# Two transformer blocks: the first FFN matrix product in pairs of elements, as seven block products instead of eight

## The chip, the core and the metric

The kernel runs on one core of a Trainium2 chip. The metric is the device time of one execution in microseconds (us). A core has five engines that work side by side, each through its own instructions in order: TensorE (PE in the profile; the loading of its weights is PEld), VectorE (DVE), ScalarE (ACT), GpSimd (POOL) and SyncE (SP), which in this kernel does nothing but issue DMAs. Where an instruction waits for another engine, all that stands behind it on its own engine waits too.

## What is computed

The input `x` holds 16 elements of 256 tokens by 256 channels, all in fp32. It passes through two layers, and each layer has three parts: self-attention, cross-attention to `ctx_768`, and an FFN. Cut to the part that is changed:

```python
# layer 0 (layer 1 likewise, with weights, norms and modulation of its own)
ffn_in = layernorm(x) * (1.0 + g(cond)) + b(cond)      # per element
h = gelu(ffn_in @ ff_w1 + ff_b1, approximate=False)    # 256 -> 1024
x = h @ ff_w2 + ff_b2 + x                              # 1024 -> 256
```

The pairs of factor and addend (the "modulation") come from one conditioning vector per element.

## The kernel before

The work is cut into six phases: self-attention, cross-attention and FFN of layer 0 (p0, p1, p2), then those of layer 1 (p3, p4, p5). A phase goes through the 16 elements, b0 to b15. An attention job has two steps and an FFN job four, s = 0 to 3. One loop over all steps writes the orders of all engines by hand (`manual_schedule`): what the loop calls first comes first on each engine it touches.

**Preparing an element.** An element's input goes through a chain on several engines. `prepare_moments` takes mean and variance on DVE. `prepare_norm` takes the root on GpSimd (L330), normalizes on DVE (L338), turns 32x32 blocks on DVE (L348) and makes SP issue four DMAs to DRAM (L353, `turned`). `prepare_fetch` makes SP issue four DMAs back (L363, `fetched`). `prepare_input` applies factor and addend, one half on ACT (L396) and one on GpSimd (L397), and leaves `hT`, channels on the partitions. All DMAs of the kernel are issued from SP in program order.

**The FFN before.** The first matrix stands as two tiles `w10` and `w11` (L82's `w_a` in layer 0 and `w_b` in layer 1). `ffn_hidden(job, s)` makes 256 of the 1024 outputs for the 256 tokens of one element in one PSUM bank. `product` (L82) is one 128x128 weight block against a row of columns, written as four matmuls of 32 outputs. Two gelus on ACT (L704) move the bank to SBUF. After four steps the element has its 1024 hidden values. The output product of the element before is made meanwhile: `fold_inner` (L736) adds up five combinations of hidden blocks on DVE at s0, and `finish_folded` (L738) makes seven block products with them at s2 and adds the result to `x` on DVE (L750 to L757). Its weights are combined once for a phase by `fold_weights` (L727, five DVE additions, at s1 of b0). So the output product already takes seven block products for eight; the hidden product takes all eight.

**The borders.** The last element of cross-attention of layer 0 has its sums made (`sum_up`) and its rows scaled (`scale`, L627) while the first FFN elements run; its output product (`finish`, L775) comes at FFN b1, s3. The last self- and FFN products of a phase are made in the next phase's first steps.

**The modulations of layer 1.** Three times in layer 0's FFN, at b2, b5 and b8, a modulation is made: its weights are loaded by SP at s0; at s3 16 matmuls (L199), a copy on ACT (L204), a transpose on DVE (L206) and 16 small DMAs issued by SP (L210, `turned_b`). They are put to use one element later (DVE, L173 to L177). The sixteen are issued so:

```python
for q in range(4):
    for g in range(4):
        nc.sync.dma_start(out=turned[32 * q : 32 * q + 32, g // KC, g % KC, :],
                          in_=blocks[32 * g : 32 * g + 32, q, 0:NB])
```

In the four steps of an FFN element the loop calls, for the elements ahead:

```python
if s == 1 and after is not None:
    prepare_fetch(after)          # two ahead
if s == 1 and third is not None:
    prepare_moments(third); prepare_norm(third)
if s == 3 and after is not None:
    prepare_input(after)
```

## Time and profile before

| what | value |
|---|---|
| median of 3 runs | 2196.24 us (2194.89 to 2197.59) |
| profiled execution | 2198.64 us |
| its span | 2196.8 us |
| granted TensorE clock, mean | 0.999 |
| layer 0: self-attention, cross-attention, FFN | 615, 638, 213 us |
| layer 1: both attentions, FFN | 472, 217 us |

The span is what the hardware profiler shows of the execution, from the first to the last instruction; the profiled execution's own time is 1.84 us longer. The five stages follow each other from about 42 us on; before that the weights and constants arrive. The profile's page gives for each engine its busy time and share, and for each group of instructions its line, its operation with output and input tile, the count, the mean duration and the idle time ahead of it. In a timeline a row is a run of like instructions: start, duration, engine, line, operation, count, and in brackets the idle time before and who ended it. Every matmul of the program shows as two records.

### The profile page before, as it was taken

The page shows a single profiled execution, that of the slowest core. Times are in us where ns is not written, and L with a number is a line of the kernel's source. Part 1 is how long each engine was busy: PE and PEld are TensorE (multiplying, and loading weights), DVE is VectorE, ACT ScalarE, POOL GpSimd, SP SyncE. Part 2 cuts the span into 40 slices and gives each one's busy share as a digit, 9 for nine tenths or more (in the row PEclk, how much of TensorE's full clock was granted, in tenths as well). Part 3 has the DMA queues.
Part 4 walks back from the last instruction along what each step waited for, and adds up shares of the span by engine and source line. Part 5 has one row for each costly group of instructions (what it writes and reads, how often), then busy time and mean ns, then how long its engine had stood idle before and what let it go on. Part 6 is the DMA issues. An engine that isn't in the chain of part 4 may idle for free.

```text
span 2196.8 us, 110836 instructions
## 1 busy us (share of the span) xinstructions
PE 2180.7 (99%) x50505; PEld 1431.6 (65%) x50505; DVE 1660.6 (76%) x3120; ACT 837.5 (38%) x1307; POOL 1071.6 (49%) x1033
## 2 busy tenths in 40 slices
PE   9999999999999999999999999999999999999998
PEld 5666666666665666666665668776656656657887
DVE  5886776777788899888899876664777777777654
ACT  3323323323233333333323332234666666663322
POOL 3766656656657867676676752221222232222220
PEclk9999999999999999999999999999999999999999
DMA  6110110110132221221212123221221232223221
GB/s 192 47 39 22 24 40 23 24 41 22 26 85 72 67 65 35 47 54 40 60 35 59 26 71 88 46 54 29 62 43 42 55 93 59 62 52 86 61 62 37
DMA packets 309321, 117.83 MB, mean 54 GB/s; under 512 B 245652, under 2 KB 292073, under 8 KB 308713
## 3 DMA queue, kind: packets, MB, share of 16 engines
q1 hardware_dynamic: 308840, 110.64, 21.1%
q8 instruction: 397, 6.50, 1.2%
q14 instruction: 84, 0.68, 0.1%
HBM read 77.14 MB, written 33.29 MB: 50 GB/s over the span
## 4 chain that ended last, share of the span: by engine, by line
PE 91%; DVE 3%; POOL 2%; DMA 1%; issue 1%; SPq 0%; ACT 0%; DVEq 0%; POOLq 0%; ACTq 0%
PE banks L82 59%; PE banks L569 15%; PE banks L638 9%; PE banks L654 5%; PE banks L505 1%; PE banks L472 1%; DVE m L526 1%; POOL raw L627 1%; POOL qk L534 1%; DMA spread<-sums_seen 0%; POOL folded L736 0%; DMA sums_seen<-inv 0%; DVE both L590 0%; DVE rows L603 0%; DVE squares L596 0%
## 5 line engine op out<-in xcount | busy, mean ns | idle before, releaser
L581 ACT ACTIVATE pr<-banks 128x1024 f32<-128x1024 f32 x576 | 487.6, 937 | 416.7 <-PE banks L569 211.5
L534 POOL TENSOR_TENSOR qk<-m,m 128x512 f32<-128x512 f32 x256 | 347.5, 1377 | 307.7 <-DVE m L526 199.6
L526 DVE TENSOR_TENSOR m<-banks,rope 128x512 f32<-128x512 f32 x512 | 324.2, 679 | 86.4 <-POOL qk L534 80.8
L590 DVE TENSOR_TENSOR both<-pr 128x512 f32<-128x512 f32 x256 | 222.7, 884 | 107.7 <-ACT pr L581 107.4
L645 ACT COPY raw<-banks 128x512 f32<-128x512 f32 x128 | 75.1, 587 | 468.6 <-PE banks L638 443.3
L569 PE MATMUL banks<-qk 32*64 32x256 f32 x8192 | 241.4, 378 | 4.0 <-DVE x L753 2.8
L638 PE MATMUL banks<-pr,v 128*32 128x256 f32 x4096 | 233.2, 379 | 0.0
L569 PEld LDWEIGHTS banks<-qk 32*64 32x64 f32 x8192 | 184.9, 131 | 64.6 <-issue 28.7
L704 ACT ACTIVATE g<-banks,cols 128x256 f32<-128x256 f32 x256 | 106.4, 472 | 273.0 <-PE banks L82 261.4
L638 PEld LDWEIGHTS banks<-pr,v 128*32 128x32 f32 x4096 | 132.9, 110 | 88.6 <-ACT pr L581 0.7
L82 PE MATMUL banks<-folded_w,folded 128*32 128x128 f32 x5856 | 176.2, 273 | 1.7 <-POOL folded L736 1.1
L627 POOL TENSOR_TENSOR raw<-raw,spread 128x512 f32<-128x512 f32 x128 | 162.8, 1304 | 19.0 <-DMA spread<-sums_seen 17.7
L82 PEld LDWEIGHTS banks<-folded_w,folded 128*32 128x32 f32 x5856 | 164.0, 110 | 3.1 <-POOL folded L736 2.2
L596 DVE STREAM_TRANSPOSE squares<-both 128x1024 f32<-128x1024 f32 x128 | 159.4, 1245 | 4.4
L603 DVE TENSOR_REDUCE rows<-squares 128x32 f32<-128x1024 f32 x128 | 155.5, 1215 | 2.2
L689 POOL TENSOR_TENSOR oT<-oT,spread 128x256 f32<-128x256 f32 x64 | 45.7, 736 | 209.8 <-DVE spread L688 209.8
L654 PE MATMUL banks<-pr,wide_v 128*32 128x256 f32 x2048 | 134.4, 379 | 1.1 <-ACT pr L581 1.1
L82 PE MATMUL banks<-hT,wk_sa 128*32 128x256 f32 x2048 | 135.3, 382 | 0.0
L330 POOL TENSOR_TENSOR rstd<-ve,neg_half 128x2 f32<-128x2 f32 x95 | 73.3, 772 | 125.9 <-DVE ve L328 122.5
L423 POOL TENSOR_TENSOR x<-x,bo_b 128x256 f32<-128x256 f32 x96 | 73.2, 782 | 125.8 <-DVE xh L338 125.8
L82 PE MATMUL banks<-hT,wq_ca 128*32 128x256 f32 x2048 | 133.9, 379 | 0.0
L82 PE MATMUL banks<-hT,wq_sa 128*32 128x256 f32 x2048 | 133.9, 379 | 0.0
(162 smaller groups left out, 3667.0 us busy)
## 6 DMA issues: line engine op xcount, KB each, us to landing
turned<-blocks SPq DMA_DIRECT2D x380, 64.0 KB
fetched<-turned SPq DMA_DIRECT2D x380, 64.0 KB
spread<-sums_seen SPq DMA_DIRECT2D x128, 128.0 KB
x<-in_x SPq DMA_DIRECT2D x16, 256.0 KB
fetched_c<-turned_c SPq DMA_DIRECT2D x64, 64.0 KB
cT<-in_ctx_turned SPq DMA_DIRECT2D x16, 256.0 KB
out<-x SPq DMA_DIRECT2D x16, 256.0 KB
ctx<-in_ctx SPq DMA_DIRECT2D x16, 192.0 KB
```

Of the source, the lines that this page charges most:

```text
L82: nc.tensor.matmul(out[cut], lhsT[:, cut], rhs, start=start, stop=stop)
L526: nc.vector.tensor_tensor(m, pq, rope[:, s : s + 1, :].to_broadcast([P, 2, N]), ALU.mult)
L534: nc.gpsimd.tensor_tensor(r, x, y, (ALU.subtract, ALU.add)[out])
L569: nc.tensor.matmul(banks[64 * g : 64 * g + 64, at + h, t * N : (t + 1) * N], lhs, rhs, start=(half == 0), stop=(half == 1 or job["layer"] ...
L581: nc.scalar.activation(pr[:, one], sc[:, one], AF.Exp, scale=0.125 if job["layer"] == 0 else 0.25)
L590: nc.vector.tensor_tensor(job["both"][:, 2 * p : 2 * p + 2, :], pr[:, :, 0, :], pr[:, :, 1, :], ALU.add)
L596: nc.vector.transpose(job["squares"].rearrange("p b k -> p (b k)"), job.pop("both").rearrange("p h n -> p (h n)"))
L603: nc.vector.tensor_reduce(job["rows"][:, u, :], job.pop("squares"), AX.X, ALU.add)
L627: nc.gpsimd.tensor_tensor(part, part, spread[:, u : u + 1, :].to_broadcast([P, 2, N]), ALU.mult)
L638: nc.tensor.matmul(o[32 * h : 32 * h + 32, half, :], v[:, t, col : col + 32], prs[h // 2][:, h % 2, t, :], start=(t == 0), stop=(t == NT - 1),
L654: nc.tensor.matmul(o[32 * h : 32 * h + 32], v[:, t, 4 * c + h, 32 * e : 32 * e + 32], prs[h // 2][:, h % 2, t, :], start=(t == 0), stop=(t ...
L704: nc.scalar.activation(g[:, c, :], ph[:, c, :], AF.Gelu, bias=column(w["b1"], 2 * u + c))
```

## The change

The FFN elements go in pairs (b0 and b1, b2 and b3, and so on), eight pairs in each layer, and a pair's eight steps are q = 0 to 7. The two elements' `hT` stand side by side in one tile. The hidden product is cut in two by two blocks: the 1024 outputs in two halves j, the 256 inputs in two halves k, the 256 tokens of each element in two halves t. One `block` is 512 outputs by 128 inputs by 128 tokens of both elements, four `product`s or 16 matmuls of 256 columns, in two banks. Seven blocks replace eight, named here A1 to A7 in the order of a steady pair: A1 at q0 (in the banks `main`), A2 at q0 (`side`, banks 6 and 7), A3 at q0 (`other`), A4 at q1, A5 at q3, A6 at q5 and A7 at q6. `main` and `other` change places from pair to pair. Around them:

- `split_weights`: four sums of 128x512 weight blocks on GpSimd, once for each layer; `split_input`: four sums of 128x256 on GpSimd per pair, made at q4 and q6 of the pair before.
- `kept` copies of running sums in `main` from PSUM to SBUF on ACT, and `join`s on DVE that add a bank to such a copy and leave the hidden values before gelu.
- gelus then run on SBUF, in halves: those of outputs 0 to 511 one pair later (q0 and q1), those of outputs 512 to 1023 at q3 and q6.
- The output products of a pair's elements come at q2 and q4 of the next pair, in banks 0 and 1 and with an order of their own; `fold_inner` is divided, three sums on DVE and two on GpSimd. After the last pair both elements' products follow each other.
- Fetches and inputs of the elements ahead move: in a steady pair the next pair's first element is fetched at q0 and its input made at q2, the second's at q3 and q4. `enter_ffn` at the last step of an attention phase prepares the first pair and fetches the third element.
- The first pair has no output products of its own phase behind it; its A6 comes at q1, its A3 at q5, `fold_weights` at q3. The last pair has A3 at q1, and its output products of the pair before at q4 and q7.
- The late output product of cross-attention moves to the second pair's q1. The modulations are made at q2 of the pairs of b2, b4 and b6. The product of the last but one FFN element of layer 0 moves to layer 1's first attention phase as a plain product.

The core of the diff:

```diff
+        into = None
+        if job["kind"] == "ffn":
+            if b % 2 == 0:
+                job["pair"] = work.tile([P, KC, 2, N], F32, tag="v", name=f"hT_{key}")
+            else:
+                job["pair"] = jobs[job["index"] - 1]["pair"]
+            into = job["pair"][:, :, b % 2, :]
...
-    def ffn_hidden(job, u):
...
+    def split_weights(ph):
+        w = ph["w"]
+        a = [[w[f"w1{j}"][:, k, :] for k in range(2)] for j in range(2)]
+        if ph["layer"] == 0:
+            s12, s34 = wtile([P, 2, 512], "wk0", "split_a0"), wtile([P, 2, 512], "wk1", "split_a1")
+        else:
+            both = wtile([P, 4, 512], "wv", "split_b")
+            s12, s34 = both[:, 0:2], both[:, 2:4]
+        s1, s2, s3, s4 = ph["split"] = s12[:, 0], s12[:, 1], s34[:, 0], s34[:, 1]
+        nc.gpsimd.tensor_tensor(s1, a[1][0], a[1][1], ALU.add)
+        nc.gpsimd.tensor_tensor(s2, s1, a[0][0], ALU.subtract)
+        nc.gpsimd.tensor_tensor(s3, a[0][0], a[1][0], ALU.subtract)
+        nc.gpsimd.tensor_tensor(s4, a[0][1], s2, ALU.subtract)
+    def input_blocks(job):
+        return [[job["pair"][:, k, :, t * P : (t + 1) * P] for t in range(2)] for k in range(2)]
+    def split_input(job, part):
+        b = input_blocks(job)
+        t = work.tile([P, 2, 2, P], F32, tag="hT", name=f"split_{job['key']}_{part}")
+        job.setdefault("split", []).extend((t[:, 0], t[:, 1]))
+        t1, t2, *_ = job["split"]
+        if part == 0:
+            nc.gpsimd.tensor_tensor(t1, b[0][1], b[0][0], ALU.subtract)
+            nc.gpsimd.tensor_tensor(t2, b[1][1], t1, ALU.subtract)
+        else:
+            nc.gpsimd.tensor_tensor(t[:, 0], b[1][1], b[0][1], ALU.subtract)
+            nc.gpsimd.tensor_tensor(t[:, 1], b[1][0], t2, ALU.subtract)
+    def gelu(job, j, cut, src=None):
+        dst = job["halves"][j]
+        for i in range(4):
+            nc.scalar.activation(
+                dst[:, i, cut], dst[:, i, cut] if src is None else src[:, i, :], AF.Gelu,
+                bias=column(job["phase"]["w"]["b1"], 4 * j + i),
+            )
+    every_token, first_half, second_half = slice(0, N), slice(0, P), slice(P, N)
+    def ffn_hidden(job, q):
+        key, ph, mate = job["key"], job["phase"], jobs[job["index"] + 1]
+        a = [[ph["w"][f"w1{j}"][:, k, :] for k in range(2)] for j in range(2)]
+        b = input_blocks(job)
+        s1, s2, s3, s4 = ph["split"]
+        odd = job["b"] // 2 % 2
+        before = jobs[job["index"] - 1]
+        pending = (jobs[job["index"] - 2], before) if before["kind"] == "ffn" else None
+        main, other, side = (2 + 2 * odd, 4 - 2 * odd, 6)
...
+        def block(at, left, right, start):
+            for i in range(4):
                 product(
-                    ph[:, c, :], w[f"w1{u // 2}"][:, k, (2 * (u % 2) + c) * P : (2 * (u % 2) + c + 1) * P], job["hT"][:, k, :],
-                    k == 0, k == KC - 1,
+                    banks[:, at + i // 2, i % 2 * N : i % 2 * N + N].rearrange("p (e n) -> p e n", e=2),
+                    left[:, i * P : (i + 1) * P], right, start and i % 2 == 0, True, True,
                 )
...
+        def join(j, t, at, kept):
+            for e, one in enumerate((job, mate)):
+                for half in range(len(kept)):
+                    n = 4 // len(kept)
+                    nc.vector.tensor_tensor(
+                        one["halves"][j][:, n * half : n * half + n, t * P : (t + 1) * P],
+                        parted(at)[:, n * half : n * half + n, e, :], kept[half][:, :, e, :], ALU.add,
+                    )
...
+        final = mate["b"] == NB - 1
+        def fold(one):
+            fold_inner(one, nc.vector, 2, 1, 6)
+            fold_inner(one, nc.gpsimd, 5, 7)
+        if q == 0:
+            for one in (job, mate):
+                one["halves"] = [
+                    work.tile([P, 4, N], F32, tag=("pr", "part")[odd], name=f"g_{one['key']}_{j}", bufs=4)
+                    for j in range(2)
+                ]
+            block(main, a[0][0], b[0][0], True)
+            job["first"] = kept("both", 0)
+            if pending:
+                gelu(pending[0], 0, every_token)
+                fold(pending[0])
+            block(side, s1, job["split"][0], True)
+            if pending and not final:
+                block(other, a[0][1], b[1][0], True)
+                join(0, 0, other, job.pop("first"))
+        elif q == 1:
+            block(main, s2, job["split"][1], False)
+            second = kept("squares", 1)
+            if pending:
+                job["second"] = second
+                gelu(pending[1], 0, every_token)
+                if final:
+                    block(other, a[0][1], b[1][0], True)
+                    join(0, 0, other, job.pop("first"))
+            else:
+                block(0, s4, b[1][1], True)
+                join(0, 1, 0, second)
+                for e, one in enumerate((job, mate)):
+                    sums = one["halves"][0][:, :, second_half]
+                    nc.vector.tensor_tensor(sums, parted(side)[:, :, e, :], sums, ALU.add)
+        elif q == 3:
+            if pending and not final:
+                fold(pending[1])
+            block(main, s3, job["split"][2], False)
+            third = []
+            for half in range(2):
+                t = work.tile([P, 2, 2, P], F32, tag="m0", name=f"kept_{key}_2{half}")
+                nc.scalar.copy(
+                    t.rearrange("p i e n -> p i (e n)"), flat(main)[:, 2 * half : 2 * half + 2, :]
+                )
+                third.append(t)
+            join(1, 1, side, third)
+            for one in (job, mate):
+                gelu(one, 1, second_half)
+        elif q == 5 and pending:
+            block(side, s4, b[1][1], False)
+            join(0, 1, side, job.pop("second"))
+        elif q == 5:
+            block(other, a[0][1], b[1][0], True)
+            join(0, 0, other, job.pop("first"))
+        elif q == 6:
+            block(main, a[1][1], job["split"][3], False)
+            if final:
+                fold(pending[1])
+                for one in (job, mate):
+                    gelu(one, 0, every_token)
+            for e, one in enumerate((job, mate)):
+                gelu(one, 1, first_half, parted(main)[:, :, e, :])
+                one["parts"] = [h[:, 2 * i : 2 * i + 2, :] for h in one["halves"] for i in range(2)]
...
-    def finish_folded(job, at):
+    def finish_folded(job, at, order):
         x, weights, hidden = xs[job["b"]], job["phase"]["folded"], job.pop("folded")
-        hurry = len(at) == 3
-        first, second, third = (bank(i, 4, P) for i in (at if hurry else (*at, at[1])))
+        first, second = (bank(i, 4, P) for i in at)
         places = {5: first[:, 0], 2: first[:, 1], 4: first[:, 2], 3: first[:, 3],
-                  1: third[:, 0], 7: second[:, 1], 6: second[:, 2]}
-        for m in (3, 6, 4, 5, 2, 1, 7) if hurry else places:
+                  1: second[:, 0], 7: second[:, 1], 6: second[:, 2]}
+        for m in order:
...
+    def enter_ffn(j):
+        prepare_fetch(jobs[j + 3])
+        prepare_input(jobs[j + 2])
+        for part in range(2):
+            split_input(jobs[j + 1], part)
+        prepare_norm(jobs[j + 4])
...
-        late = prev if not ffn else jobs[j - 2] if prev["kind"] == "ffn" else None
+        late = prev if not ffn else jobs[j - 3] if job["b"] == 2 else None
...
-        if ffn and layer0 and job["b"] in (2, 5, 8):
-            at = phases[3 + job["b"] // 3]
+        if ffn and layer0 and job["b"] in (2, 4, 6):
+            at = phases[2 + job["b"] // 2]
             if s == 0:
                 at["make_mod"] = at["mod_load"]()
-            if s == 3:
+            if s == 2:
                 make_mod = at
-        if ffn and layer0 and job["b"] in (3, 6, 9) and s == 3:
-            at = phases[2 + job["b"] // 3]
+        if ffn and layer0 and job["b"] in (3, 5, 7) and s == 3:
+            at = phases[2 + job["b"] // 2]
             at["mod"] = at["mod"]()
...
         if ffn:
...
-                stage_a(then[0], 0, next_bank())
...
+            q = s + 4 * (job["b"] % 2)
+            one = job if q < 4 else prev
+            before = jobs[one["index"] - 1]
+            previous = before["kind"] == "ffn"
+            if q in (0, 4) and third is not None and (previous or q == 4):
+                prepare_moments(third)
+            for ahead in (after if previous else third,) if q == 0 else (third,) if q == 3 and previous else ():
+                if ahead is not None:
+                    prepare_fetch(ahead)
+            if q == 0 and not previous and before["layer"] == 1:
+                normalize(before)
+            then = attention(i + 3, 1)
+            if q == 5 and then:
+                stage_a(then[0], 0, 3)
                 for t in range(NT):
-                    layer1_values(then[0], next_bank(), t)
+                    layer1_values(then[0], 2 - t, t)
+            ffn_hidden(one, q)
+            if previous:
+                for at, n in zip((4, 7) if one["b"] == NB - 2 else (2, 4), (2, 1)):
+                    if q == at:
+                        finish_folded(jobs[one["index"] - n], (0, 1), (4, 3, 2, 5, 1, 6, 7))
+            else:
+                if q == 1 and layer0:
+                    sum_up(before, 5)
+                if q == 6 and not layer0:
+                    finish(before, 0)
+                if q == 3:
+                    fold_weights(job["phase"])
+            if late is not None and q == 1:
+                finish(late, 1)
             if make_mod:
-                make_mod["mod"] = make_mod["make_mod"](next_bank())
...
+            ahead = {2: after, 4: after} if previous else {2: after, 3: third}
+            if ahead.get(q) is not None:
+                prepare_input(ahead[q])
+            if q in (4, 6) and nxt is not None and nxt["kind"] == "ffn":
+                split_input(nxt, q // 6)
+            if q == 6 and not previous and layer0:
+                scale(before)
         elif layer0:
             then = attention(i + 1, 0)
+            if leaving and s == 1 and nxt["kind"] == "ffn":
+                split_weights(nxt["phase"])
+                prepare_norm(third)
...
+            if job["p"] == 3 and job["b"] == 1 and s == 0:
+                finish(jobs[j - 3], at + 1)
...
-    fold_inner(jobs[-1], nc.vector, 6, 5, 2, 1, 7)
-    finish_folded(jobs[-1], (1, 2, 3))
+        if job["last"] and s == 3 and job["b"] == 7:
+            count_outside()
+    for n in (2, 1):
+        fold_inner(jobs[-n], nc.vector, 2, 1, 6, 7, 5)
+        finish_folded(jobs[-n], (2 * n - 4 + 4 * (n == 1), 2 * n - 3 + 4 * (n == 1)), (4, 3, 2, 1, 6, 7, 5))
```

## The prediction, written before the changed kernel ran

> **What bounds the kernel now.** I read the page's busy shares and the shares of its chain first, then timelines of the FFN stages, engine by engine. The page:
>
> ```profile
> PE 2180.7 (99%) x50505; PEld 1431.6 (65%) x50505; DVE 1660.6 (76%) x3120; ACT 837.5 (38%) x1307; POOL 1071.6 (49%) x1033
> ...
> PE 91%; DVE 3%; POOL 2%; DMA 1%; issue 1%; SPq 0%; ACT 0%; DVEq 0%; POOLq 0%; ACTq 0%
> ```
>
> TensorE is the bound: busy for 2180.7 of 2196.8 us, so work taken from it counts in full, and every wait that the new order gives it counts in full too. The change is thus a balance of saved matmuls against new waits. A timeline of layer 0's FFN around the second modulation (start, duration, engine, line, count, idle before):
>
> ```profile
> 1375.79 0.70 PE L199 MATMUL banks<-mod_b,condT 128*16 128x128 f32 x15
> ...
> 1377.57 12.24 SPq L210 DMA_DIRECT2D turned_b<-blocks_b  x16
> ...
> 1381.41 2.01 PE L82 MATMUL banks<-w_a,folded 128*32 128x128 f32 x63
> ...
> 1387.73 7.07 PE L82 MATMUL banks<-hT,w_a 128*32 128x256 f32 x125
> ...
> 1389.92 1.91 SPq L363 DMA_DIRECT2D fetched<-turned  x4
> ...
> 1394.43 2.01 PE L82 MATMUL banks<-w_a,folded 128*32 128x128 f32 x63
> ...
> 1394.54 0.60 ACT L396 ACTIVATE hT<-fetched,add_a,fac_a 128x256 f32<-128x256 f32 x1 [4.03 <-DMA fetched<-turned]
> ```
>
> Two output products begin 13.02 us apart (1394.43 - 1381.41): a steady element has no gap. SP is held for 12.24 us by sixteen tiny transfers, 0.77 us each; the fetch behind them starts when they are through, and ACT waits for it (4.03). In this order that hurts nobody, since the element fetched is needed later. The entry of layer 0's FFN, on GpSimd and DVE:
>
> ```profile
> 1283.19 5.96 POOL L627 TENSOR_TENSOR raw<-raw,spread 128x512 f32<-128x512 f32 x4
> ...
> 1285.64 2.37 DVE L590 TENSOR_TENSOR both<-pr 128x512 f32<-128x512 f32 x2
> ...
> 1289.39 1.30 DVE L590 TENSOR_TENSOR both<-pr 128x512 f32<-128x512 f32 x2
> ...
> 1295.84 0.69 DVE L775 TENSOR_TENSOR x<-banks,x 128x512 f32<-128x512 f32 x1 [1.49 <-PE banks L82]
> ...
> 1303.01 3.64 DVE L727 TENSOR_TENSOR folded_w<-w_a 128x512 f32<-128x512 f32 x5
> ```
>
> The same two additions take 2.37 us while GpSimd multiplies and 1.30 us when it has done: what GpSimd is given more of, DVE pays here.
>
> **The saving.** In the 125 records from 1387.73 on, 62.5 matmuls of 256 columns take 6.70 us up to 1394.43: 0.107 each, 0.429 a product. A hidden product of one element (64 matmuls) is 6.86, the output product the rest of 13.02, 6.16. A pair has 7 blocks of 4 products where it had 8: 4 x 0.429 = 1.72 us less, for 16 pairs -27.4. A block is 1.72.
>
> **Steady pairs.** A pair lasts 7 x 1.72 + 2 x 6.16 = 24.3 us on TensorE. DVE has in it six folds (0.64 each), two sets of output additions (2.6), joins (4 x 0.69, 4 x 0.42) and two norms (2.7), 19.2 in all; ACT about 12.6 (two copies of 1.04, two of 0.59, gelus at 0.42 and 0.27, affines); GpSimd 14 (four folds at 1.4, four splits at 0.76, affines, roots). None is over 24.3, and placed by hand the tightest operand, A3's turn behind the eight small gelus, has about 1 us to spare. I take 0; bounds 0 and +0.5 a pair.
>
> **The modulations: the decider.** In a pair that makes one, the sixteen DMAs stand at q2 and the fetch of the next pair's second element at q3, directly behind them on SP. Behind that fetch ACT and GpSimd hold its affines (q4), behind these ACT's gelus of A7 and GpSimd's splits. A1 of the next pair now reads both elements side by side, so it waits for this second one. From the modulation's first matmul to the end of that affine the trace has 1394.54 + 0.60 - 1375.79 = 19.35 us (1.78 to the first DMA, 12.35 to the fetch, 4.62 to ACT, 0.60). The third modulation gives 19.26 and the first 24.39, with four weight loads between that now come later. TensorE meanwhile has the 16 matmuls (0.65), A5, an output product, A6 and A7: 0.65 + 3 x 1.72 + 6.16 = 11.97. So it waits 7.4 us, three times: +22.2. Bounds: 5.9 each if other small waits fill 1.5 us of it, 12.4 each by the longest chain: 17.7 to 37. I take the two agreeing chains.
>
> A rule speaks for less: the Trainium skill, page "DMA: Bandwidth & Descriptors", section "Anatomy of one DMA — SWDGE (gpsimd) path", puts about 2 us on a DMA but only some 50 ns of it on dispatch. By it (an estimate, for a path that SP's queue need not share) sixteen are issued in 0.8 us, the chain is under 9 and the sum would be -10.7. The row of 12.24 for sixteen decides otherwise.
>
> **The entries.** Layer 0: TensorE enters at about 1295.3 and its seven blocks and the sums (0.4) would end at 1307.7. But four splits of the weights on GpSimd stand beside the additions (the 2.37 row), and the norm of b2 waits on DVE for a root that GpSimd makes only after L627's 5.96; so the addition that stood at 1295.84 ends at about 1300. After it DVE has moments, the joins and fold_weights (3.64), and the join of A3 stands behind them, to about 1315.5. The second pair's A1 writes A3's banks: it starts at 1315.6, +8.0 (6.5 if the splits cost DVE nothing, 10 if the output addition is later still). Layer 1: TensorE enters at 1979.7; its blocks and the attention's product (1.72) would end at 1993.4. The second pair needs b3, whose fetch is issued in the entry behind b2's and lands near 1996.7; affine and join take it to 1998.6: +5.2 (4 to 6.5).
>
> **The end.** Timeline of the last products:
>
> ```profile
> 2188.38 1.94 PE L82 MATMUL banks<-folded_w,folded 128*32 128x128 f32 x64
> ...
> 2188.72 0.42 DVE L750 TENSOR_TENSOR x<-x,banks 128x256 f32<-128x256 f32 x1 [1.06 <-PE banks L82]
> ...
> 2190.84 0.42 DVE L757 TENSOR_TENSOR x<-banks,x 128x256 f32<-128x256 f32 x1
> ```
>
> Before, the additions run into the last products and end 1.16 us after them. Now b15's folds stand behind b14's five additions on DVE, so TensorE waits about 1.6, and as product 5 comes last all five additions (2.55) follow it, 1.4 more: +3.0 (2.5 to 3.7).
>
> **The rest.** b14 of layer 0 as a plain product is 16 products, 6.86 for 6.16, +0.7, and its addition holds a bank for another +0.5 (0 to 0.7). The exp at the border to layer 1 kept TensorE 1.3 us; now about 0.6, as the gelus end sooner: -0.7 (-1.3 to 0). The late cross product moves past nothing that waits; the splits for layer 1 go beside layer 1's attention, where GpSimd has 131 us of work in 472: 0.
>
> **Sum.** -27.4 + 8.0 + 5.2 + 22.2 + 3.0 + 1.2 - 0.7 = +11.5. The profiled execution took 2198.64 (span 2196.8 and 1.84 around it), so 2210.1 by its measure; it lies 2.40 above the median, so 2207.7 against that. With the terms' ends, and 26 for the modulations, which is about half way from the value taken to the upper end, this case runs from +2.7 to +20: 2199 to 2216. Differences under 0.2% (4.4 us) can't be told from none here.
>
> **Rivals.** (1) Faster: the fetch is in time. It decides when the chain from modulation to affine is under 15.5 us: then three waits of 3.6 make 10.7, what the saving leaves over the other terms (27.4 - 16.7). With no wait at all (11.97) the sum is -10.7, 2185.5; with the entries covered too, 2172. It would take DMAs issued at about 0.45 us, as SP's row of 0.47 for a single bias load shows, in place of 0.77. Against: all three rows of sixteen are 12.06 to 12.65. Chance 0.18, and 0.10 for a partial cover that ends within 0.2%. (2) More waits: DVE and GpSimd have 33 us of work per 24.3 side by side, and where they hinder each other as in the 2.37 row, each of 14 later pairs loses 0.5 to 1 us: +7 to +14 on top, 2215 to 2222. Against: the steady pair's slack of 1 us. Chance 0.18. (3) That the saving isn't there: a pair's blocks are 7 x 16 matmuls in the program's order against 128; I give it nothing. The main case keeps 0.54.
>
> **Range and chances.** From 2183, which takes in all of rival 1 but the covered entries (0.08 left out), to 2218, which leaves out the upper part of rival 2 (0.10). Faster 0.18, same 0.10, slower 0.72.
>
> **What would show it.** Of the changed profile: blocks in rows of 1.72; the sixteen DMAs still over 12 us and a fetch behind them; three idle times of TensorE of about 7 us ended by ACT's affine ahead of the pairs of b4, b6 and b8; one of 6 to 8 at about 1308, ended by a join on DVE; one of about 5 in layer 1's first pair; a stage of layer 0's FFN near 213 - 13.7 + 30 = 229 us and of layer 1's near 217 - 13.7 + 8.2 = 211.5. If the three idle times are under 3.6 us each, or TensorE's busy time doesn't fall by about 27, the forecast is wrong.

## The result and the profile after

The changed kernel takes 2218.36 us (median of 4 runs, 2217.78 to 2222.47) against 2196.62 for the kernel before on the same chip: ratio 1.0105, 95% interval 1.0091 to 1.0118. It is slower, by 21.7 us; the forecast was +11.5, and 2218 at most. The profiled execution took 2217.78, with a span of 2216.0.

The page of the changed kernel, busy shares and chain:

```profile
PE 2166.4 (98%) x49897; PEld 1420.2 (64%) x49897; DVE 1729.5 (78%) x3191; ACT 909.3 (41%) x1499; POOL 1209.6 (55%) x1161
...
PE 90%; DVE 3%; SPq 2%; POOL 2%; issue 1%; DMA 1%; ACT 0%; DVEq 0%; POOLq 0%; ACTq 0%
```

TensorE has 608 records fewer, but only 14.3 us less busy time where the blocks saved are worth 27.4: some matmuls have become slower. SP, which had no share of the chain, now has 2%. What TensorE waited for (us in total, times, longest):

```profile
PE banks L76 <- ACT hT L390: 16.8, 3, 6.0
PE banks L76 <- DVE folded L877: 5.7, 2, 4.4
PE banks L76 <- DVE g L772: 3.8, 1, 3.8
PE banks L76 <- ACT g L735: 2.5, 1, 2.5
PE banks L76 <- POOL split L725: 2.1, 2, 1.6
```

The first line is the forecast gate, three times; the third is layer 0's entry, the fourth layer 1's. The second holds a wait of 4.4 us that the forecast did not have. The timeline of the second modulation and of the next pair's start, in the changed kernel (A1, A2, A3 are the rows of L76 from 1383.94 on):

```profile
1366.90 0.61 PE L193 MATMUL banks<-mod_b,condT 128*16 128x128 f32 x16
...
1368.28 11.32 SPq L204 DMA_DIRECT2D turned_b<-blocks_b  x16
...
1376.90 1.90 PE L76 MATMUL banks<-split,w_a 128*32 128x256 f32 x32
...
1379.71 1.91 SPq L357 DMA_DIRECT2D fetched<-turned  x4
...
1383.28 0.60 ACT L390 ACTIVATE hT<-fetched,add_a,fac_a 128x256 f32<-128x256 f32 x1 [9.74 <-DMA fetched<-turned]
...
1383.94 3.64 PE L76 MATMUL banks<-hT,w_a 128*32 128x256 f32 x32 [5.14 <-ACT hT L390]
1387.35 2.93 PE L76 MATMUL banks<-split,split_a 128*32 128x256 f32 x32
1390.12 1.90 PE L76 MATMUL banks<-hT,w_a 128*32 128x256 f32 x32
```

The chain is the one of the prediction: sixteen DMAs, the fetch, the affine, A1. But A1 then takes 3.64 us and A2 2.93, and only A3 has the 1.90 of any other block. The table by stretches of time shows why (length, busy time of PE, PEld, DVE, ACT and POOL, granted clock, DMA share, GB/s):

```profile
1378.50:1384.00 5.50, 0.36 (x12) 0.06 (x8) 3.27 (x14) 0.72 (x2) 0.59 (x2) 0.87 0.36 97
1384.00:1389.50 5.50, 5.50 (x56) 2.52 (x60) 0.00 (x0) 3.74 (x12) 4.82 (x7) 0.51 1.01 270
```

After the idle stretch the granted clock is 0.51: TensorE works at half speed for the next 5.5 us. The kernel before, in which TensorE never waits longer than 1.3 us, shows 1.00 through both of its FFNs. The border to layer 1 in the changed kernel, in the rows of four engines:

```profile
1515.14 1.92 PE L76 MATMUL banks<-folded_w,g 128*32 128x128 f32 x64
...
1515.46 0.56 POOL L391 TENSOR_SCALAR hT<-fetched,fac_b,add_b 128x256 f32<-128x256 f32 x1 [7.54 <-PE banks L76]
1515.96 1.84 POOL L310 MEMSET wide_v<- 128x1024 f32 x2
...
1516.95 0.76 DVE L490 TENSOR_TENSOR wide_v<-banks,bv_b 128x256 f32<-128x256 f32 x2 [5.59 <-POOL wide_v L310]
...
1520.15 2.90 DVE L877 TENSOR_TENSOR folded<-g,g 128x512 f32<-128x512 f32 x2
...
1521.42 3.64 PE L76 MATMUL banks<-w_a,folded 128*32 128x128 f32 x64 [4.36 <-DVE folded L877]
```

GpSimd stands for 7.54 us before an affine whose buffer A7 still reads; behind it stands a memset, behind that DVE's addition, on DVE behind that the fold, and TensorE waits for the fold. A steady pair, for comparison, from one A1 to the next:

```profile
1444.86 1.90 PE L76 MATMUL banks<-hT,w_a 128*32 128x256 f32 x32
...
1469.18 1.90 PE L76 MATMUL banks<-hT,w_a 128*32 128x256 f32 x32
```

24.32 us, where the prediction had 24.3: the saving is there, in full.

From the first FFN matmul of layer 0 to the end of the span the kernel before takes 2196.8 - 1295.2 = 901.6 us and the changed one 2216.0 - 1292.8 = 923.2: +21.6. The account, with "slow clock" as TensorE's busy time times one minus the granted clock, added up over stretches of half a microsecond:

| term | forecast | idle | slow clock | measured |
|---|---|---|---|---|
| seven blocks for eight | -27.4 | | | -27.4 |
| entry of layer 0 | +8.0 | 1.59 + 1.38 + 0.29 + 3.84 | 1.7 | +8.8 |
| three modulations | +22.2 | 16.8 | 7.2 | +24.0 |
| border to layer 1 | -0.2 | 4.36 | 2.3 | +6.7 |
| plain product | +0.7 | | | +0.7 |
| entry of layer 1 | +5.2 | 0.48 + 2.46 | 0 | +2.9 |
| the end | +3.0 | 1.34 + 0.94 | | +2.3 |

The sum of the measured terms is +18.0; the other 3.6 are in none of its rows. Of these, 1.1 are waits of half a microsecond and less. The rest fits this estimate: a row of matmuls ends 0.18 after the point where the next could begin (1.90 for a block that takes 1.72 in sequence), so each of the 14 new waits costs 0.18 more than the idle time shown, 2.5 in all. The first and the fifth row are the forecast's own figures: the saving is supported by the steady pair of 24.32, the plain product was not measured by itself. The border's forecast is -0.7 and the +0.5 of the held bank. The end's 0.94 is the time from TensorE's last matmul to the end of the span, 7.38 for 6.44. The changed kernel's FFN also begins 2.4 us sooner (1292.8 for 1295.2), as in every run of a kernel made from it; two waits in cross-attention are shorter. That was not followed up.

### The profile page after: what moved, and what is told of

Its sections match the earlier page's. It is cut to its first block, busy times and chain, and to the rows that moved or that the text cites. A ratio compares the mean times of both kernels' runs of the same rounds, so it can differ in the third digit from the quotient of the medians.

```text
span 2216.0 us, 110006 instructions
## 1 busy us (share of the span) xinstructions
PE 2166.4 (98%) x49897; PEld 1420.2 (64%) x49897; DVE 1729.5 (78%) x3191; ACT 909.3 (41%) x1499; POOL 1209.6 (55%) x1161
## 4 chain that ended last, share of the span: by engine, by line
PE 90%; DVE 3%; SPq 2%; POOL 2%; issue 1%; DMA 1%; ACT 0%; DVEq 0%; POOLq 0%; ACTq 0%
PE banks L76 58%; PE banks L570 15%; PE banks L639 9%; PE banks L655 5%; SPq L204 2%; PE banks L506 1%; PE banks L473 1%; DVE m L527 1%; POOL qk L535 1%; POOL raw L628 0%; DMA fetched<-turned 0%; DVE both L591 0%; SPq L357 0%; DVE g L772 0%; POOL folded L877 0%
## 5 line engine op out<-in xcount | busy, mean ns | idle before, releaser
L628 POOL TENSOR_TENSOR raw<-raw,spread 128x512 f32<-128x512 f32 x128 | 163.3, 1310 | 21.6 <-DMA spread<-sums_seen 21.0
L76 PE MATMUL banks<-folded_w,folded 128*32 128x128 f32 x5760 | 169.4, 273 | 0.2 <-POOL folded L877 0.2
L76 PEld LDWEIGHTS banks<-folded_w,folded 128*32 128x32 f32 x5760 | 159.1, 110 | 0.9 <-POOL folded L877 0.4
L76 PE MATMUL banks<-hT,wk_sa 128*32 128x256 f32 x2048 | 134.8, 381 | 0.0
L76 PE MATMUL banks<-hT,wq_sa 128*32 128x256 f32 x2048 | 134.0, 379 | 0.0
L76 PE MATMUL banks<-hT,wq_ca 128*32 128x256 f32 x2048 | 134.0, 379 | 0.0
L479 ACT COPY v<-banks 128x512 f32<-128x512 f32 x128 | 70.3, 593 | 143.1 <-PE banks L76 81.5
L570 PE MATMUL banks<-q,k 32*64 32x256 f32 x4096 | 128.3, 381 | 0.4 <-DVE x L897 0.4
```

What stands on the lines that cost most here:

```text
L76: nc.tensor.matmul(out[cut], lhsT[:, cut], rhs, start=start, stop=stop, skip_group_check=read_between)
L570: nc.tensor.matmul(banks[64 * g : 64 * g + 64, at + h, t * N : (t + 1) * N], lhs, rhs, start=(half == 0), stop=(half == 1 or job["layer"] ...
L628: nc.gpsimd.tensor_tensor(part, part, spread[:, u : u + 1, :].to_broadcast([P, 2, N]), ALU.mult)
```

## The experiments

The theory: each new wait adds its idle time, and where it is long enough, matmuls at half clock behind it. The rivals stand with each expectation. All kernels start from the changed one. In differences of medians to the kernel before on the same chip: changed kernel +21.7.

**1. The fetch ahead of the sixteen DMAs.**

```diff
-        if ffn and layer0 and job["b"] in (3, 5, 7) and s == 3:
-            at = phases[2 + job["b"] // 2]
+        if ffn and layer0 and job["b"] in (4, 6, 8) and s == 3:
+            at = phases[1 + job["b"] // 2]
             at["mod"] = at["mod"]()
...
-            for ahead in (after if previous else third,) if q == 0 else (third,) if q == 3 and previous else ():
+            mod_pair = ffn and layer0 and one["b"] in (2, 4, 6)
+            for ahead in (after if previous else third,) if q == 0 else (third,) if q == 3 and previous and not mod_pair else ():
...
             if make_mod:
+                prepare_fetch(jobs[j + 3])
                 make_mod["mod"] = make_mod["make_mod"](5 - 2 * (job["b"] // 2 % 2))
```

> The fetch of the next pair's second element stands on SP ahead of the sixteen small DMAs of a modulation, and the modulation is put to use half a pair later; all the rest is as changed. Theory (the sixteen DMAs hold that fetch, and TensorE's clock falls after each wait): the three waits for ACT's affine of 5.9, 5.3 and 6.2 us go, and with them the slow matmuls behind them (1.4 + 2.7 + 3.0), together 24.4: 2218.4 - 24.4 = 2194. Rival (the waits belong to the affine or to the transfers themselves): a wait of 3 us or more stays in each, 2204 or more.

Measured: 2201.74, ratio 1.0026 (1.0015 to 1.0038), +5.6. No wait for ACT's affine is left in the FFN, and no slow clock behind the modulations: the gate is shown. But 8 of the 24 us did not come. TensorE's new waits, from timelines of this run:

```profile
1364.96 1.95 PE L76 MATMUL banks<-w_a,folded 128*32 128x128 f32 x64 [1.08 <-DVE folded L877]
...
1387.66 1.10 PE L193 MATMUL banks<-mod_b,condT 128*16 128x128 f32 x14 [1.65 <-DMA mod_b<-in_L_xcond_Wmod]
...
1393.99 1.08 PE L76 MATMUL banks<-w_a,folded 128*32 128x128 f32 x32 [0.78 <-POOL folded L877]
...
1419.67 1.08 PE L76 MATMUL banks<-w_a,folded 128*32 128x128 f32 x32 [1.06 <-POOL folded L877]
```

4.6 us in all, and at layer 1's entry the clock fell this time (1.7). The first of them comes from the factors on DVE, made while GpSimd folds:

```profile
1361.31 0.27 DVE L168 SCALAR_TENSOR_TENSOR fac_b<-add_b,cols 128x32 f32<-128x32 f32 x1
1361.62 1.23 DVE L169 SCALAR_TENSOR_TENSOR add_b<-add_b,cols 128x32 f32<-128x32 f32 x1
1362.88 1.20 DVE L170 TENSOR_TENSOR add_b<-add_b,cols 128x32 f32<-128x32 f32 x1
```

Operations of 128x32 that take 0.19 us in the changed kernel's FFN, where the factors are made at another time, take 1.2 here. The Trainium skill, page "SBUF — State Buffer", section "Who interferes with whom", has a cause for such rows: DVE and GpSimd share a pair of ports under an exclusive lock, so one of them stands while the other holds it.

**2. The same, with the modulations spread.** Made at b2, b6 and b10, their factors at q5 of the next pair.

```diff
-        if ffn and layer0 and job["b"] in (2, 4, 6):
-            at = phases[2 + job["b"] // 2]
+        if ffn and layer0 and job["b"] in (2, 6, 10):
+            at = phases[3 + job["b"] // 4]
...
-        if ffn and layer0 and job["b"] in (3, 5, 7) and s == 3:
-            at = phases[2 + job["b"] // 2]
+        if ffn and layer0 and job["b"] in (5, 9, 13) and s == 1:
+            at = phases[2 + job["b"] // 4]
```

> The fetch stands ahead of the sixteen DMAs again, the three modulations are made two pairs apart (at b2, b6 and b10 in place of b2, b4 and b6), and their factors are computed after an output product's additions, at q5 of the next pair, where GpSimd makes no folds. Theory: what fetch_first still lost in layer 0's FFN (1.1 for DVE's fold behind the factors, 1.65 for the third modulation's weights, 1.8 for GpSimd's folds) goes: 4.5 less than its 2201.7, 2197. Rival (these waits come from the steady pair itself): 2202.

Measured: 2195.45, ratio 1.0000 (0.9991 to 1.0009), +0.6. The factors no longer delay a fold and the third modulation does not wait for its weights; one wait of 1.39 for GpSimd's fold stays. So the place of the modulations, on SP and in the order of pairs, and what hangs on it, was worth 21 of the 21.7 us by which the changed kernel lost.

**3. Filling the waits.** To separate the idle time from the slow clock, the waits behind the modulations are filled with blocks whose result nobody reads, two as written here and then three.

```diff
+            if q == 7 and layer0 and one["b"] in (2, 4, 6):
+                blocks_of = input_blocks(one)
+                for _ in range(2):
+                    for i4 in range(4):
+                        product(
+                            banks[:, i4 // 2, i4 % 2 * N : i4 % 2 * N + N].rearrange("p (e n) -> p e n", e=2),
+                            one["phase"]["w"]["w10"][:, 0, i4 * P : (i4 + 1) * P], blocks_of[0][0], i4 % 2 == 0, True, True,
+                        )
```

> Changed kernel, and in each of the three waits behind a modulation TensorE is given two extra blocks (3.4 us of work that nobody reads) after A7. The gate of the fetch stays. Theory of the clock (idle times of over about 3.4 us lower the granted clock to 0.5 for a while, shorter ones do not, as the 2.5 us wait in layer 1 shows): the next pairs begin at the same moment as before but at full clock, 7.1 us less: 2211.3. Rival (the slow matmuls come from the DMA traffic or from the operands' arrival): the clock falls as before, 2218.

> Changed kernel with three extra blocks (5.15 us) in each of the three waits behind a modulation, so that under 1.5 us of idle time are left in each. fill_gaps left 2.5 to 2.8 and still lost 1.7 to the clock in one of three. Theory: no clock is lost behind the modulations; the next pairs begin when the fetch has come, as in the changed kernel, 2218.4 - 7.1 = 2211.3. Rival (the clock falls because of the transfers): 1.4 to 3.0 lost in each as before, 2218.

Measured: 2215.28, ratio 1.0089 (1.0074 to 1.0105), and 2214.16, ratio 1.0086 (1.0072 to 1.0099). The A1s behind the three waits with two blocks:

```profile
1353.21 1.93 PE L76 MATMUL banks<-hT,w_a 128*32 128x256 f32 x32 [2.78 <-ACT hT L390]
...
1384.30 2.44 PE L76 MATMUL banks<-hT,w_a 128*32 128x256 f32 x32 [2.68 <-ACT hT L390]
...
1416.99 1.93 PE L76 MATMUL banks<-hT,w_a 128*32 128x256 f32 x32 [2.52 <-ACT hT L390]
```

and with three:

```profile
1355.10 1.93 PE L76 MATMUL banks<-hT,w_a 128*32 128x256 f32 x32 [1.16 <-ACT hT L390]
...
1386.43 1.93 PE L76 MATMUL banks<-hT,w_a 128*32 128x256 f32 x32 [1.20 <-ACT hT L390]
...
1417.30 1.93 PE L76 MATMUL banks<-hT,w_a 128*32 128x256 f32 x32 [0.73 <-ACT hT L390]
```

Three blocks leave no slow clock behind the modulations, in place of 7.2 us; two leave 1.7 in one case of three. The transfers are the same, so the slow matmuls come from the idle time, not from the DMAs. The medians gained less than the 7.1 expected: 2.6 and 1.7 in the difference to before, with intervals that overlap the changed kernel's. In the profile with three blocks the clock fell in two places where it had not fallen in the changed kernel's (1.6 at the entry of layer 0, 1.7 at that of layer 1), and the span is 2.9 shorter. So the mechanism is shown by the rows, and its sum in one execution is partly chance.

What decides between waits of like length can be read from the traces. Within each of the thirteen traces (before, after and every experiment), all changes of the clock lie whole multiples of 3.41 us apart. They fall on a grid of slots that runs through the execution, each time from another starting point. In the kernel with two blocks, the slot with most of each wait, and under it the next slot (columns as in the table above):

```profile
1351.45:1354.86 3.41, 1.65 (x32) 1.05 (x36) 0.83 (x5) 2.30 (x9) 2.10 (x4) 1.00 0.55 100
1354.86:1358.27 3.41, 3.41 (x72) 2.04 (x67) 0.35 (x1) 2.97 (x7) 3.41 (x6) 1.00 0.72 224
1382.17:1385.58 3.41, 1.28 (x24) 0.81 (x28) 1.51 (x8) 1.93 (x7) 1.73 (x3) 1.00 0.80 235
1385.58:1389.00 3.42, 3.42 (x38) 1.74 (x32) 0.00 (x0) 2.88 (x8) 3.42 (x6) 0.50 1.10 277
1412.89:1416.30 3.41, 1.58 (x31) 1.02 (x23) 2.01 (x10) 0.00 (x0) 0.00 (x0) 1.00 0.35 91
1416.30:1419.71 3.41, 2.72 (x52) 1.69 (x56) 0.00 (x0) 3.32 (x10) 3.17 (x5) 1.00 0.39 63
```

TensorE was busy for 1.65, 1.28 and 1.58 us of these slots, and only behind the 1.28 did the clock fall. The same line divides all traces: of 8247 whole slots at full clock, up to TensorE's last matmul, the 35 with 1.34 us of busy TensorE or less are each followed by a slot at half clock, and none of the others is, the least of which has 1.56. The clock came back after every one of the 35 slots at half clock with 2.68 us or more of work, and after none of the nine with 2.57 or less. So a slot with about 2 us of idle time, in one wait or in two, lowers the clock. From this follows an estimate: a wait of up to 1.85 us (3.41 - 1.56) passes anywhere if no other is near it, one of over 4.1 us (twice 3.41 - 1.34) passes nowhere, and in between the place in the grid decides. The ends of matmuls are modelled in the profile, so the bounds are good to about a tenth.

**4. The input at the border later.**

```diff
-            ahead = {2: after, 4: after} if previous else {2: after, 3: third}
+            into_attention = nxt is not None and nxt["kind"] == "attn"
+            ahead = {2: after, 6 if into_attention else 4: after} if previous else {2: after, 3: third}
```

> Changed kernel, with the input of layer 1's second element (last pair of layer 0's FFN) called at q6 in place of q4. Theory: GpSimd's affine waits for a buffer that A7 still reads, and behind it stand the memset of the values, on that DVE's join and folds, on these the output product; the 4.4 us wait for DVE's fold goes and with it 2.3 of slow clock: 2218.4 - 6.7 = 2211.7. Rival (DVE is simply behind with its folds): 2217 to 2218.

Measured: 2213.72, ratio 1.0080 (1.0067 to 1.0094), +17.6. The wait at the border:

```profile
1516.67 2.23 PE L76 MATMUL banks<-w_a,folded 128*32 128x128 f32 x64 [0.43 <-DVE folded L877]
```

0.43 for 4.36, and no slow clock there. Against the expected 6.7 the difference to before fell by 4.1; this execution lost 1.5 to the clock at the entry of layer 0, where the other had not.

**5. The additions of the output weights later.**

```diff
-                if q == 3:
+                if q == 6:
                     fold_weights(job["phase"])
```

> Changed kernel, with the five additions of the output weights of a layer (3.1 us on DVE) moved from q3 to q6 of the first pair, behind the join of A3. Theory: the join ends some 3 us sooner, the wait of 3.84 ahead of layer 0's second pair falls to about 1, when the next input is there, and the clock stays up (1.7): 4.5 less, 2213.9. Rival (the second pair's input is what comes last): 2218.

Measured: 2215.65, ratio 1.0090 (1.0075 to 1.0106), +19.5. The wait of 3.84 became one of 1.06 for the next input, and the clock stayed up; but the late cross product, reached sooner, now waits for GpSimd's scaling, four times:

```profile
1310.05 1.93 PE L76 MATMUL banks<-hT,w_a 128*32 128x256 f32 x32 [1.06 <-ACT hT L390]
...
1318.01 1.07 PE L76 MATMUL banks<-wo_ca,raw 128*32 128x256 f32 x16 [0.85 <-POOL raw L628]
...
1323.12 4.52 PE L76 MATMUL banks<-wo_ca,raw 128*32 128x256 f32 x80 [0.61 <-POOL raw L628]
```

In layer 1 the entry's wait fell from 2.46 to 1.33 and two for folds of 0.52 and 1.25 came after it.

**6. The end in another order.** b15's folds stand on DVE ahead of b14's additions, and product 5 is made fourth.

```diff
+        if between is not None:
+            between()
         blocks = x.rearrange("p t (n i) -> p (t n) i", i=P)
...
+    fold_inner(jobs[-2], nc.vector, 2, 5, 1, 6, 7)
+    finish_folded(
+        jobs[-2], (0, 1), (4, 3, 2, 5, 1, 6, 7), lambda: fold_inner(jobs[-1], nc.vector, 2, 5, 1, 6, 7)
+    )
+    finish_folded(jobs[-1], (2, 3), (4, 3, 2, 5, 1, 6, 7))
```

> Changed kernel, and at the end b15's folds come ahead of b14's additions on DVE, and product 5 is made fourth in place of last. By the sum of the prediction the end cost 3.0 (1.6 of waiting, 1.4 of additions): TensorE's last wait of 1.34 goes and two additions in place of five follow the last product, about 2.9 less: 2215.5. Rival (the way of the output sets the end): 2218.

Measured: 2213.85, ratio 1.0084 (1.0070 to 1.0097), +19.0. In the changed kernel the end reads

```profile
2204.03 1.08 PE L76 MATMUL banks<-w_b,folded 128*32 128x128 f32 x32 [1.34 <-DVE folded L877]
...
2207.54 1.06 PE L76 MATMUL banks<-w_b,folded 128*32 128x128 f32 x32
...
2208.67 0.42 DVE L890 TENSOR_TENSOR x<-x,banks 128x256 f32<-128x256 f32 x1 [2.29 <-PE banks L76]
...
2210.64 0.42 DVE L897 TENSOR_TENSOR x<-banks,x 128x256 f32<-128x256 f32 x1
```

and in this one

```profile
2201.93 2.80 PE L76 MATMUL banks<-folded_w,folded 128*32 128x128 f32 x96
...
2202.97 0.69 DVE L895 TENSOR_TENSOR x<-banks,x 128x512 f32<-128x512 f32 x1
2204.80 0.42 DVE L898 TENSOR_TENSOR x<-banks,x 128x256 f32<-128x256 f32 x1 [1.14 <-PE banks L76]
2205.26 0.42 DVE L899 TENSOR_TENSOR x<-banks,x 128x256 f32<-128x256 f32 x1
```

No wait, and two additions after the last product. From layer 1's first FFN matmul to the end of the span it is 2210.7 - 2004.16 = 206.5 for 2216.0 - 2005.61 = 210.4, 3.9 less. Of these, 3.1 lie behind the start of the last pair's A6 (28.0 for 31.1), which is the end; the rest lies ahead of it, where the order is the same.

**7. All together.** Experiments 2, 4 and 5 with the late cross product at q3 of the second pair; then with the end of 6 and with two of the four sums of weight blocks made after the first input split; then with the late product at q1 again; then with layer 1's additions of weights back at q3.

```diff
-            if late is not None and q == 1:
+            if late is not None and q == 3:
                 finish(late, 1)
...
+        def rest():
             nc.gpsimd.tensor_tensor(s4, a[0][1], s2, ALU.subtract)
             nc.gpsimd.tensor_tensor(s3, a[0][0], a[1][0], ALU.subtract)
```

> mods_spread with the input at the border of the layers called later, the additions of the output weights moved to q6 of the first pairs, and the late cross product moved from q1 to q3 of the second pair (so that it does not wait for GpSimd's scaling). Theory (the saving of 27.4 is all there, and each wait adds to it by itself): 2197 - 6.7 - 4.5 = 2186, under the kernel before. Rival (waits hand on: one taken away shows the next): 2192 or more.

> four_undone with the end of tail_folds_first and with the last two sums of weight blocks for layer 0 made after the first input split (the wait of 1.6 ahead of A2). Theory: 2186 - 2.9 - 1.5 = 2182. Rival as in four_undone: 2188 or more.

> all_undone with the late cross product at q1 again, as in the changed kernel. Theory (GpSimd's scaling of 5.9 us stands ahead of its two folds; the late product of 6.9 us at q1 covers them, at the price of 2.7 us of waits inside it): the waits of 2.29 and 2.40 for the folds and the 2.5 of slow clock behind them go, 2.7 come: 2189 - 4.5 = 2184.5. Rival (the folds are late in any order): 2189.

> The same, but in layer 1 the five additions of the output weights stay at q3. Layer 1 then waits 2.5 us once (and sometimes 1.7 more by the clock) in place of 1.27 + 0.51 + 1.24: within 2 us of late_product_back.

Measured:

| kernel | median us | ratio to before (95%) | difference us |
|---|---|---|---|
| four undone | 2193.58 | 0.9994 (0.9985 to 1.0003) | -1.3 |
| all undone | 2189.01 | 0.9971 (0.9961 to 0.9981) | -5.8 |
| late product back at q1 | 2184.20 | 0.9954 (0.9941 to 0.9968) | -10.0 |
| and layer 1's weights at q3 | 2183.70 | 0.9950 (0.9936 to 0.9964) | -10.5 |

The first missed its expectation, as the rival said, by a wait that my own move had made:

```profile
1326.86 1.93 PE L76 MATMUL banks<-w_a,folded 128*32 128x128 f32 x32 [5.24 <-POOL folded L877]
```

GpSimd folds after its scaling of some 6 us, and without the late product of 6.9 us in front TensorE is at the folds too soon. The second missed its 2182 for the same reason: waits of 2.29 and 2.40 for the folds stand in that place, with 2.5 us of slow clock. With the late product back at q1 that wait is gone, 1.9 to 2.9 us of small ones stand inside the product, and the clock is not lowered any more (0.999 over the span, as before). The last two kernels agree within half a microsecond, as expected. Both beat the kernel before by about 10 us. The best kernel's page:

```profile
PE 2155.1 (99%) x49897; PEld 1418.4 (65%) x49897; DVE 1727.0 (79%) x3191; ACT 909.9 (42%) x1499; POOL 1214.1 (56%) x1161
```

TensorE's busy time is 25.6 less than before (2180.7), the saving but for 2 us. The profiled span of 2181.5 is 15.3 shorter than that of before, so 10.3 us more of it are idle: short waits at the entries, folds and borders that the order with eight blocks did not have. The medians, which stand for more than one execution, differ by 10.5.

## Why the prediction was wrong

The direction held, and of the three largest terms two held and the third, the modulations, in its total only. The time lies 0.4 us above the range's end. Two steps failed, one in the price of a wait and one in the list of waits.

**"Every wait that the new order gives it counts in full too": a wait counts for more.** The sum took each wait as idle time at full clock. In the changed kernel's FFN of layer 0 the slow clock adds 11.1 us (1.7 at the entry, 7.2 behind the modulations, 2.3 at the border); in the kernel before it is 0. Without it the time would be about 2207 (2218.4 - 11.1, an estimate). That this is the forecast's 2207.7 is luck: the idle time behind the modulations was 5.4 less than forecast and that at layer 1's entry 2.3 less, while the border took 4.6 more and 3.6 were in no term. I had the waits of 5 to 8 us on paper, and no row of before could show what they do, since its longest is 1.3. The Trainium skill does: page "TensorE: Matmul & The Clock Gate", section "Part 1: The HAM clock gate", says that the clock halves after an idle window of about 3.4 us and comes back after about 3.4 us of work, and that the window runs free of the kernel. Weighed against these runs: all 27 waits of over 3.8 us in the changed kernel and the experiments lost 1.3 to 3.0 us, and in the changed kernel the clock then stood at 0.50 for 3.41 or 6.83 us, one slot of the grid or two. Of eleven waits between 2.46 and 2.78 us four lost 1.7, and two waits of 1.5 and 1.4 us close behind each other lost as much in three runs of nine. So the free window of 3.4 us is what the traces show (experiment 3), but it need not be idle: up to 1.34 us of work in it did not keep the clock up, and here the measurement decides.

**"The exp at the border to layer 1 kept TensorE 1.3 us; now about 0.6 ...: -0.7": the border became +6.7.** The wait for the exp itself stayed (1.25 for 1.29 us), and a wait that the sum did not have came ahead of it: 4.36 us and 2.3 of slow clock. I looked at the gelus there and not at what the moved input does on GpSimd: its affine writes a buffer that A7 still reads, and memset, addition, joins and fold stand behind it (experiment 4). What is queued behind a waiting instruction was named for the fetch and not for this one.

**The upper end was reckoned too low.** The 26 us for the modulations are called "about half way" from 22.2 to 37; half way is 29.6. With it the main case would have ended at +24, above the measured +21.7, but without the slow clock being in it.

The other steps:

- The saving: 24.32 a pair for 24.3, right. TensorE's busy time, which was to fall by about 27, fell by 14.3, because it holds the 11.1 of slow clock; without them it fell by 25.4.
- Steady pairs at 0: right, nothing over 0.4 us; rival 2 did not come, though DVE's folds beside GpSimd's work take up to 1.78 us for 0.68. (DVE's 19.2 us a pair add up to 18.9 from the figures named, which changes nothing.)
- The modulations: the mechanism, the place and the number of waits right; the chain ran 17.0 to 17.9 us and not 19.35, as the sixteen began 1.4 after the matmul for 1.78 and the fetch landed in 3.6 for 4.6. So the idle time was 16.8 and not 22.2, and the slow clock of 7.2 took the place of the difference. The sixteen took 11.32 to 12.13 us; the 50 ns of dispatch on the page quoted there, for another path, do not describe SP's issue here. (The 16 matmuls of a modulation are 8 in the program and 16 records; the 0.65 us are of the records and stand.)
- The entry of layer 0: 7.1 of waits, its last as named (join behind the additions of weights, experiment 5), and 1.7 of clock: 8.8 for 8.0. Layer 1's: 2.9 for 5.2, by DVE and ACT and not by b3's fetch, so the size and the cause were off.
- The end: 2.3 for 3.0, with the wait 1.34 for 1.6. The additions end 2.5 us after the last product, and in the kernel before 0.94 (2191.26 - 2190.32) and not 1.16, so they took 1.5 for 1.4; the way out behind them was 0.6 shorter.
- Rival 1's price for a covered gate, -10.7 with all other terms left in: with the gate alone moved the kernel came to +0.6. Most of that gap of 11.3 is the border's wait (4.3) and the slow clock (5.8 in that execution), the same terms that the sum lacked.

## What to carry to other kernels

A wait of the busiest engine has two prices, its length and what the clock does after it: where a change turns many short waits into a few long ones, count the slow matmuls behind each too, and fill or shorten waits until no stretch of 3.4 us holds about 2 us of idle time. When an operation is moved, follow the buffer it writes as well as the data it reads: a prepared input that waits for a buffer holds up all that its engine has behind it. A burst of small DMAs on a queue that also carries what the next step needs belongs behind that transfer, and a product that covers a slow engine must not be moved without something in its place.

## What the runs showed of the hardware

What lowered TensorE's clock was not the length of a wait alone, but a slot of the grid of 3.41 us with 1.34 us of work or less (35 of 35; none of 8212 with 1.56 or more). That 10 to 15 us of matmuls that nobody reads cost nothing measurable (experiment 3: medians 2.6 and 1.7 lower, intervals that overlap) was the least expected. Sixteen DMAs of 32 rows by 64 bytes hold SP for 11.3 to 12.7 us in the rows read, before and after, 0.7 to 0.8 us each, while single DMAs of weights take 0.42 to 0.61. DVE's additions of 128x32 go from 0.19 to 1.2 us, and its folds of 128x512 from 0.68 to 1.78, while GpSimd folds or scales beside them.
